# The round of a local transformer in another order: values at its head, scores in two halves

## The chip, the cores and the metric

The kernel runs on one core of a Trainium2 chip. A core has five engines that run side by side, each with its own queue of instructions: TensorE (PE, matmuls; PEld is its loading of weights), VectorE (DVE), ScalarE (ACT), GpSimd (POOL) and SyncE (SP, which issues transfers). An instruction waits in its queue until the semaphores that it names are high enough, and everything behind it on that queue waits with it. PE writes to PSUM, a memory of eight banks; DVE and ACT read results from there. The metric is the time on the device in microseconds (us), the median over runs. All times below are in us unless ns is written.

## The reference

The reference takes `x` of four sequences of 512 tokens with 128 features and adds eight blocks to it: cross attention, a mixture of experts, cross attention, a quantised feed-forward block with a convolution, a windowed cross attention, a transformer of six layers with local attention, cross attention, and a second mixture of experts. The change lies in the transformer of six layers alone. In each layer it computes (cut to what matters):

```
def attn_layer(x, Wqkv, qs, ksc, Wo):
    q, k, v = jnp.split(x @ Wqkv, 3, -1)          # 16 heads of 64
    q = l2norm(q) * qs;  k = l2norm(k) * ksc
    q = q * cos * scale + rotate_half(q) * sin * scale
    k = k * cos / scale + rotate_half(k) * sin / scale
    # windows of 32 queries, each sees its own 32 keys and the 32 before them, masked
    attn = jax.nn.softmax(8.0 * einsum(q, k), -1)
    return einsum(attn, v) @ Wo
def ffn_layer(x, g, bln, W1, b1, W2, b2):
    a, gate = jnp.split(layernorm(x, g, bln) @ W1 + b1, 2, -1)
    return a * jax.nn.gelu(gate) @ W2 + b2
for i in range(6):
    x = attn_layer(shift_tokens(x), Wqkv[i], q_scale[i], k_scale[i], Wo[i]) + x
    x = ffn_layer(shift_tokens(x), ln_g[i], ln_b[i], W1[i], b1[i], W2[i], b2[i]) + x
```

`shift_tokens` moves half of the features by one token. All of it is computed in 32-bit floats.

## The kernel before

The kernel has three stages. The first and the last (first, middle and last part) are lists of pieces that a planner puts into an order by estimated costs; the change does not touch them. Between them stands `local_transformer` (from line 1804), whose order is written out by hand: `tc.manual_schedule()` leaves each engine's instructions in the order of the program, and the framework adds the semaphores that the data, the buffers and the PSUM banks ask for.

The work is cut into tiles of 128 tokens: 6 layers x 4 sequences x 4 tiles, 96 tiles in all. The loop of line 2095 runs over rounds n. Round n works on three tiles at once: T (tile n), T1 (n-1) and T2 (n-2). Beside them runs the feed-forward block of a finished sequence (a "row" of four tiles), F, spread over four rounds, its phases 0 to 3. The parts of a round are:

- `queries_or_keys(T, kind, c)` (line 1835): a product of 128x128 with 128x512 for half c of the queries (kind 0) or keys (kind 1) into one of two banks "mm", and its squares on ACT. `rotate` (1847): on DVE two multiplications by tables of cosine and sine and a sum of the squares per head, on POOL the addition of the two. `normalise` (1868): inverse norms of queries and keys, with Ln and Exp on ACT between small steps on POOL, and then four multiplications on POOL.
- `values(T, x0)` (1905): two products into the banks "tr", copied by ACT to `v1`, and four to six transfers on SP that make the shifted copy `v2`; POOL sets a column of ones first. Averages read them two rounds later.
- `turned(T1, kind)` (1886): eight transposes on PE for queries or keys, copied by ACT. For keys, POOL first copies the last 32 columns of the tile before.
- `scores(T1)` (1932): eight matmuls that put the mask into the two banks "sc", and 128 small ones (64 rows, 32 columns, 64 wide) that add the scores. `softmax(T1)` (1955): maximum and subtraction on DVE, the exponential on ACT (line 1965).
- `probabilities(T2)` (1967): eight transposes of the exponentials. `average(T2, g)` (1972): 64 small matmuls with the values for four pairs of heads, into the banks "av"; `normalised(T2, g)` (1987) divides by the sums on DVE and frees these banks, which the next averages need. `attended(T2)` (1995): eight transposes of the averages. `project_out(T2)` (2001): sixteen matmuls into "av"; `residual(T2)` (2007) adds them to Y on DVE.
- `ff_stage(F, phase, second)` (2074): phase 0 transposes of Y and moments, and later in the round the norm on DVE (`ff_norm`); phase 1 transposes ("turn") and gates 0 and 1, whose Gelu runs on ACT; phase 2 gate 2, then ups 0 and 1 (DVE); phase 3 up 2, then the down product, which DVE adds to Y. All of these use the banks "sc", between two uses by scores.
- `swap` (2065): a copy on ACT with the halves of the features exchanged, once per row, for the products of the values.

All transposes of a tile go through `to_features` (617, on PE line 621), four to a bank "tr". ACT holds one set of function tables at a time: Gelu needs another set than Ln and Exp, and line 2084 loads the set for Ln and Exp again after gate 2. Exp alone and Ln alone also stand in sets of their own; a pass of the build puts a load before a function that the present set lacks.

The order of a round before is: first products of the queries, probabilities, second product, the feed-forward's first part, first averages, queries turned, keys' first product, second averages, keys turned, keys' second product, averages' transposes, scores, output product, values, the feed-forward's second part.

Of the kernel before, what the change touches and what calls it, by code (L numbers as in the profile page):

```python
# [21 lines left out]
F32 = mybir.dt.float32  # L22
# [4 lines left out]
ALU = mybir.AluOpType  # L27
# [3 lines left out]
NT = S // 128  # L31
# [241 lines left out]
def tile_kernel(ctx: ExitStack, tc: tile.TileContext, A: dict, out: bass.AP):  # L273
# [1530 lines left out]
    def local_transformer(Y, lf, lw, columns, tabs):  # L1804

        with ExitStack() as es:
# [21 lines left out]
            class Tile:  # L1828


                def __init__(self, i, b, tt):
                    self.i, self.b, self.tt = i, b, tt
                    self.rot, self.raw, self.ss = {}, {}, None
# [34 lines left out]
            def normalise(T):  # L1868
# [13 lines left out]
                for (kind, c), a in sorted(T.rot.items()):  # L1882
                    o = LH * kind + 8 * c
                    G.tensor_tensor(a, a, bc(y[:, o : o + 8], [128, 8, LD], 2), ALU.mult)  # L1884

            def turned(T, kind):
# [3 lines left out]
                t = qp.tile([128, LH // 2, lead + 128], F32, name="kT" if kind else "qT")  # L1890
                if kind and T.tt:
                    G.tensor_copy(t[:, :, 0:32], T.before.kT[:, :, 128:160])
                elif kind:
                    G.memset(t[:, :, 0:32], 0.0)
# [5 lines left out]
                if kind:  # L1900
                    T.kT = t
                else:
                    T.qT = t
# [28 lines left out]
            def scores(T):  # L1932

                T.banks = pair("sc").rearrange("p z (k d) -> p z k d", d=64)
                for w in range(4):
                    for z in range(2):
                        r = slice(64 * (z ^ (w // 2)), 64 * (z ^ (w // 2)) + 64)
                        PE.matmul(  # L1940
                            T.banks[32 * w : 32 * w + 32, z], identb[r, r.start : r.start + 32],
                            maskw[r, int(w + T.tt == 0)], start=True, stop=False,
                            skip_group_check=True,
                        )
                for k in range(LH // 2):
# [9 lines left out]
            def softmax(T):  # L1955

                P = tp.tile([128, LH // 2, 2, LD], F32, name="P", bufs=1)
                mx = small.tile([128, 2, LH // 2], F32, name="la_mx")
                V.tensor_reduce(mx, T.banks, AX.X, ALU.max)  # L1959
                V.tensor_tensor(  # L1960
                    P.rearrange("p k z d -> p z k d"), T.banks,
                    bc(mx, [128, 2, LH // 2, LD], 3), ALU.subtract,
                )
                T.P = P.rearrange("p k z d -> p k (z d)")
                SC.activation(T.P, T.P, AF.Exp, scale=8.0)  # L1965
# [56 lines left out]
            def ff_norm(F):  # L2022
                layernorm(F.xn, F.xn, F.found)
# [50 lines left out]
            def ff_stage(F, phase, second):  # L2074
                F.w1, F.w2 = loaded[F.i][2:]
                if phase == 0 and not second:
                    ff_moments(F)
                elif phase == 1:
                    ff_gate(F, 0, 1) if second else ff_turn(F)
                elif phase == 2 and second:  # L2080
                    ff_up(F, 0, 1)
                elif phase == 2:
                    ff_gate(F, 2)
                    SC.preload_act_table_set(EXP_LN)
                elif phase == 3:
                    ff_down(F) if second else ff_up(F, 2)

# [5 lines left out]
            for n in range(len(tiles) + 2):  # L2095
                T = tiles[n] if n < len(tiles) else None
                T1 = tiles[n - 1] if 0 <= n - 1 < len(tiles) else None
                T2 = tiles[n - 2] if 0 <= n - 2 < len(tiles) else None
                m, phase = divmod(n - 6, 4)
                F = rows[m] if 0 <= m < len(rows) else None  # L2100
                if T:
# [13 lines left out]
                    queries_or_keys(T, 0, 0)  # L2115
                if T2:
                    probabilities(T2)
                if T:
                    queries_or_keys(T, 0, 1)
                    rotate(T, 0, 0)  # L2120
                if F:
                    ff_stage(F, phase, False)
                if T2:
                    average(T2, 0)
                if T1:
                    turned(T1, 0)
                if T:
                    queries_or_keys(T, 1, 0)
                if T2:
                    normalised(T2, 0)  # L2130
                if T:
                    rotate(T, 0, 1)
                if T2:
                    average(T2, 1)
                if T1:
                    turned(T1, 1)
                if T:
                    queries_or_keys(T, 1, 1)
                if T2:
                    normalised(T2, 1)  # L2140
                if T:
                    rotate(T, 1, 0)
                if T2:
                    attended(T2)
                if T and T.tt == NT - 1 and n + 1 < len(tiles):
                    swap(tiles[n + 1].b)
                if T1:
                    scores(T1)
                if T:
                    rotate(T, 1, 1)  # L2150
                if T:
                    normalise(T)
                if T1:
                    softmax(T1)
# [144 lines left out]
```

## Time and profile before

| What | Value |
|---|---|
| Runs (three), median | 2462.42, from 2460.44 to 2462.8 |
| The profiled execution, its own time | 2456.04 |
| Its span, first to last instruction | 2454.2 |
| Mean granted clock of TensorE | 0.953 |
| Before the local transformer | 0 to 516.3 |
| Local transformer | 516.3 to 2172.4, 1656.1 long |
| After it | 2172.4 to 2454.2 |
| Busy in the local transformer | PE 1591.4, DVE 1326.7, POOL 1118.2, ACT 995.0 |
| Exponentials (line 1965) | 96, first at 541.8, last at 2157.2 |
| Loads of function tables on ACT | 55 of 1.28 each |

How to read the lines of the profile: a group names line, engine, operation, what it writes and reads by the program's names, shapes and count; then busy time and the mean of one in ns; then the idle time of the engine just before them, and what ended it. "issue" is time in which the engine waited for nothing that the profile shows. In a timeline the columns are start, length, engine, line, operation, tiles and count, with idle time before it in brackets. Matmuls are pipelined and their ends are modelled, so slots on PE are best read from start to start. q8 is the queue that moves instructions.

### The profile page before, as it was taken

To read this page: it belongs to the slowest core of one execution; us is meant where nothing else is said; L and a number is where in the kernel's file an instruction comes from. 1 tells how busy PE (TensorE), PEld (TensorE's weight loads), DVE (VectorE), ACT (ScalarE), POOL (GpSimd) and SP (SyncE) were. 2 spreads that over 40 slices of the span, in tenths; PEclk is the share of its full clock that TensorE was granted. 3 is DMA by queue.
4 is the path that set the end of the run, shared out by engine and by line. 5 is a ranking of instruction groups with operands and counts; after the bars stand their busy time and mean duration, and the time that the engine had idled before them with its cause. 6 is when DMAs were issued, how large, how long until landed. Compare 5 with 4: busy or idle time off the path is not lost. (4 is left out here: it accounts for less than half of the span.)

```text
span 2454.2 us, 86703 instructions
## 1 busy us (share of the span) xinstructions
PE 2228.0 (91%) x37341; PEld 1479.5 (60%) x37341; DVE 1759.3 (72%) x3896; ACT 1298.1 (53%) x2389; POOL 1338.6 (55%) x1862
## 2 busy tenths in 40 slices
PE   7958969978999999999999999999999999989676
PEld 3536734546666666666666666666666666644355
DVE  5545356866888888777887888887878788767422
ACT  3423325645666655666666666565666666525222
POOL 2141330256667676766667766766667666710433
PEclk9868989988999999999999999999999999989688
DMA  7201110016211121111211121111211111120023
GB/s 182 68 21 41 40 60 2 1 41 135 80 35 29 35 70 36 33 29 35 75 31 36 29 79 33 29 35 27 80 31 31 35 29 35 27 67 23 26 67 95
DMA packets 134298, 116.14 MB, mean 47 GB/s; under 512 B 29506, under 2 KB 102701, under 8 KB 133917
## 3 DMA queue, kind: packets, MB, share of 16 engines
q1 hardware_dynamic: 122037, 99.67, 15.8%
q0 software_dynamic: 4608, 7.35, 0.9%
q8 instruction: 296, 4.85, 0.9%
q10 hardware_dynamic: 7271, 3.58, 0.5%
q14 instruction: 86, 0.70, 0.1%
HBM read 42.84 MB, written 21.52 MB: 26 GB/s over the span
## 5 line engine op out<-in xcount | busy, mean ns | idle before, releaser
L1865 POOL TENSOR_TENSOR rc<-rc,rs 128x512 f32<-128x512 f32 x384 | 489.8, 1276 | 400.7 <-DVE rs L1855 326.3
L1842 PE MATMUL ps_mm<-wqk,y 128*128 128x512 f32 x768 | 397.2, 599 | 5.3 <-issue 3.5
L1884 POOL TENSOR_TENSOR rc<-rc,rn_y 128x512 f32<-128x512 f32 x384 | 388.6, 1044 | 7.5
L1852 DVE TENSOR_TENSOR rc<-ps_mm,tabs 128x512 f32<-128x512 f32 x384 | 262.5, 684 | 129.8 <-ACT sq L1844 126.5
L1844 ACT ACTIVATE sq<-ps_mm 128x512 f32<-128x512 f32 x384 | 231.2, 602 | 161.4 <-PE ps_mm L1842 108.0
L1855 DVE TENSOR_TENSOR rs<-ps_mm,tabs 128x512 f32<-128x512 f32 x384 | 261.5, 681 | 0.2 <-POOL rc L1865 0.2
L1864 DVE TENSOR_REDUCE ss<-sq 128x8 f32<-128x512 f32 x384 | 259.5, 676 | 0.0
L621 PE MATMUL ps_tr<-cst,rc 128*128 128x128 f32 x1536 | 210.9, 280 | 4.3 <-POOL rc L1884 4.0
L1980 PEld LDWEIGHTS ps_av<-v,PT 64*32 64x32 f32 x12288 | 138.1, 105 | 126.5 <-PE ps_tr L621 54.1
L2004 PE MATMUL ps_av<-aT,wo 128*128 128x128 f32 x1536 | 200.7, 283 | 2.4 <-issue 2.4
L2004 PEld LDWEIGHTS ps_av<-aT,wo 128*128 128x128 f32 x1536 | 181.0, 193 | 12.6 <-issue 3.9
L621 PEld LDWEIGHTS ps_tr<-cst,rc 128*128 128x128 f32 x1536 | 165.6, 142 | 24.4 <-POOL rc L1884 5.1
L1949 PE MATMUL ps_sc<-kT,qT 64*32 64x64 f32 x12288 | 148.1, 225 | 33.6 <-issue 32.9
L1980 PE MATMUL ps_av<-v,PT 64*32 64x65 f32 x12288 | 170.3, 225 | 6.2 <-DVE attn L1990 1.7
L1949 PEld LDWEIGHTS ps_sc<-kT,qT 64*32 64x32 f32 x12288 | 141.2, 105 | 44.2 <-issue 38.1
L1056 POOL DMA_INDIRECT back<-ye,to x80 | 78.8, 985 | 147.5 <-DVE ye L1170 104.0
L1842 PEld LDWEIGHTS ps_mm<-wqk,y 128*128 128x128 f32 x768 | 124.5, 192 | 56.3 <-issue 50.1
L1965 ACT ACTIVATE P<-P 128x1024 f32<-128x1024 f32 x96 | 101.4, 1057 | 97.3 <-DVE P L1960 97.3
L1876 ACT ACTIVATE rn_y<-ss 128x32 f32<-128x32 f32 x96 | 22.0, 229 | 237.9 <-POOL ss L1875 237.9
L802 ACT ACTIVATE P<-ps,deltaT 77x512 f32<-77x512 f32 x192 | 115.8, 683 | 56.7 <-PE ps L796 53.0
L1896 ACT COPY qT<-ps_tr 128x512 f32<-128x512 f32 x192 | 103.3, 589 | 74.6 <-PE ps_tr L621 74.3
L1959 DVE TENSOR_REDUCE la_mx<-ps_sc 128x16 f32<-128x1024 f32 x96 | 116.9, 1218 | 31.0 <-PE ps_sc L1949 31.0
(399 smaller groups left out, 4368.9 us busy)
## 6 DMA issues: line engine op xcount, KB each, us to landing
v<-v SPq DMA_DIRECT2D x432, 65.0 KB
v<-v SPq DMA_DIRECT2D x96, 195.0 KB
wqk<-in_L_ffn_Wqkv_dram SPq DMA_DIRECT2D x24, 256.0 KB
sent<-xn SPq DMA_DIRECT2D x2, 2210.0 KB
xe<-sent SPq DMA_DIRECT2D x16, 260.0 KB
back<-xn SPq DMA_DIRECT2D x2, 2048.0 KB
raw<-in_L_ffn_W_dram SPq DMA_DIRECT2D x8, 512.0 KB
w<-in_L_ffn_W_dram SPq DMA_DIRECT2D x16, 256.0 KB
```

The lines of the kernel that those rows point to most:

```text
L621: PE.transpose(t[:, i], src[:, i], ident)
L1842: PE.matmul(t, lhs, T.w[2 * kind + c], start=True, stop=True)
L1844: SC.activation(sq, t, AF.Square)
L1852: V.tensor_tensor(a, t, bc(T.tabs[:, 2 * kind, tt], [128, 8, LD], 1), ALU.mult)
L1855: V.tensor_tensor(r.rearrange("p h (x d) -> p h x d", x=2), t.rearrange("p h (x d) -> p h x d", x=2)[:, :, ::-1], bc(T.tabs[:, 2 * kind + ...
L1864: V.tensor_reduce(T.ss[:, kind, 8 * c : 8 * c + 8], sq, AX.X, ALU.add)
L1865: G.tensor_tensor(a, a, r, ALU.add)
L1884: G.tensor_tensor(a, a, bc(y[:, o : o + 8], [128, 8, LD], 2), ALU.mult)
L1949: PE.matmul(T.banks[32 * w : 32 * w + 32, z, k], T.qT[r, k, 32 * w : 32 * w + 32], T.kT[r, k, 32 * w : 32 * w + 64], start=False, stop=Tru ...
L1959: V.tensor_reduce(mx, T.banks, AX.X, ALU.max)
L1980: PE.matmul(T.means[32 * w : 32 * w + 32, x0, k], T.PT[r, 4 * g + k, 32 * w : 32 * w + 32], (T.v1 if w % 2 else T.v2)[r, x0, 4 * g + k], s ...
L2004: PE.matmul(t, T.wo[:, c], T.aT[:, c], start=(c == 0), stop=(c == 7))
```

## The change

The order of a round becomes a table of stages, `period`, each with the number of rounds by which its tile lags behind n, and a loop that runs through it.

- The values stand at the head of the round, after the first product of the queries; then comes the first product of the keys. The second product of the queries is the last of the four.
- `normalise` is split: the inverse norms stay at the end of the tile's own round, the four multiplications go to the head of the next one, on POOL behind the values' memsets. The copy of the keys of the tile before (`keys_before`) moves to the end of the round.
- The keys are turned ahead of the second averages.
- `scores` runs in two halves of four pairs of heads, with the averages' transposes between them.
- The residual moves to the head of the round after the output product (a lag of three), behind the feed-forward norm, which also moves to the head of the next round.
- The feed-forward's second part (gates 0 and 1, ups 0 and 1, down) moves from the round's end to its middle, between the keys' second product and the turning of the keys; on ACT it is then ahead of the round's Ln, Exp and exponential, on DVE ahead of the keys' second rotation.

One more round (99 for 98) drains the longer lag. No operation of the reference is added or left out. The diff, cut to its core:

```diff
-            def normalise(T):
+            def inverse_norms(T):
...
-                for (kind, c), a in sorted(T.rot.items()):
-                    o = LH * kind + 8 * c
-                    G.tensor_tensor(a, a, bc(y[:, o : o + 8], [128, 8, LD], 2), ALU.mult)
+                T.inv = y
+            def normalise(T, kind):
+                for c in range(2):
+                    a, o = T.rot[kind, c], LH * kind + 8 * c
+                    G.tensor_tensor(a, a, bc(T.inv[:, o : o + 8], [128, 8, LD], 2), ALU.mult)
             def turned(T, kind):
                 lead = 32 * kind
-                t = qp.tile([128, LH // 2, lead + 128], F32, name="kT" if kind else "qT")
-                if kind and T.tt:
-                    G.tensor_copy(t[:, :, 0:32], T.before.kT[:, :, 128:160])
-                elif kind:
-                    G.memset(t[:, :, 0:32], 0.0)
+                t = T.kT if kind else qp.tile([128, LH // 2, 128], F32, name="qT")
                 for c in range(2):
                     SC.copy(
                         t[:, 4 * c : 4 * c + 4, lead:],
                         to_features(T.rot[kind, c].rearrange("p (k x) d -> p k (x d)", x=2)),
                     )
-                if kind:
-                    T.kT = t
+                T.qT = T.qT if kind else t
+            def keys_before(T):
+                T.kT = qp.tile([128, LH // 2, 160], F32, name="kT")
+                if T.tt:
+                    G.tensor_copy(T.kT[:, :, 0:32], T.before.kT[:, :, 128:160])
                 else:
-                    T.qT = t
+                    G.memset(T.kT[:, :, 0:32], 0.0)
...
-            def scores(T):
...
-                for k in range(LH // 2):
+            def scores(T, g):
+                if g == 0:
+                    T.banks = pair("sc").rearrange("p z (k d) -> p z k d", d=64)
...
+                for k in range(4 * g, 4 * g + 4):
...
-            def softmax(T):
+            def largest(T):
+                T.mx = small.tile([128, 2, LH // 2], F32, name="la_mx")
+                V.tensor_reduce(T.mx, T.banks, AX.X, ALU.max)
+            def exponentials(T):
                 P = tp.tile([128, LH // 2, 2, LD], F32, name="P", bufs=1)
-                mx = small.tile([128, 2, LH // 2], F32, name="la_mx")
-                V.tensor_reduce(mx, T.banks, AX.X, ALU.max)
                 V.tensor_tensor(
                     P.rearrange("p k z d -> p z k d"), T.banks,
-                    bc(mx, [128, 2, LH // 2, LD], 3), ALU.subtract,
+                    bc(T.mx, [128, 2, LH // 2, LD], 3), ALU.subtract,
...
-            def ff_norm(F):
-                layernorm(F.xn, F.xn, F.found)
+            def ff_norm(F, phase):
+                if phase == 0:
+                    layernorm(F.xn, F.xn, F.found)
...
-            def ff_stage(F, phase, second):
-                F.w1, F.w2 = loaded[F.i][2:]
-                if phase == 0 and not second:
+            def ff_first(F, phase):
+                if phase == 0:
                     ff_moments(F)
                 elif phase == 1:
-                    ff_gate(F, 0, 1) if second else ff_turn(F)
-                elif phase == 2 and second:
-                    ff_up(F, 0, 1)
+                    ff_turn(F)
                 elif phase == 2:
                     ff_gate(F, 2)
                     SC.preload_act_table_set(EXP_LN)
+                else:
+                    ff_up(F, 2)
+            def ff_second(F, phase):
+                if phase == 1:
+                    ff_gate(F, 0, 1)
+                elif phase == 2:
+                    ff_up(F, 0, 1)
                 elif phase == 3:
-                    ff_down(F) if second else ff_up(F, 2)
+                    ff_down(F)
+            period = (
+                (ff_norm, 1),
+                (queries_or_keys, 0, 0, 0),
+                (values, 0, 0),
+                (values, 0, 1),
+                (residual, 3),
+                (queries_or_keys, 0, 1, 0),
+                (probabilities, 2),
+                (normalise, 1, 0),
+                (normalise, 1, 1),
+                (rotate, 0, 0, 0),
+                (rotate, 0, 1, 0),
+                (ff_first, 0),
+                (average, 2, 0),
+                (turned, 1, 0),
+                (queries_or_keys, 0, 1, 1),
+                (normalised, 2, 0),
+                (ff_second, 0),
+                (turned, 1, 1),
+                (average, 2, 1),
+                (rotate, 0, 1, 1),
+                (queries_or_keys, 0, 0, 1),
+                (normalised, 2, 1),
+                (scores, 1, 0),
+                (attended, 2),
+                (rotate, 0, 0, 1),
+                (scores, 1, 1),
+                (largest, 1),
+                (project_out, 2),
+                (inverse_norms, 0),
+                (keys_before, 0),
+                (exponentials, 1),
+            )
+            by_row = (ff_first, ff_norm, ff_second)
...
-            for n in range(len(tiles) + 2):
+            for n in range(len(tiles) + 3):
...
-                    queries_or_keys(T, 0, 0)
-                if T2:
-                    probabilities(T2)
-                if T:
-                    queries_or_keys(T, 0, 1)
...
-                if F and phase == 0:
-                    ff_norm(F)
-                if T:
-                    values(T, 0)
-                    values(T, 1)
-                if F:
-                    ff_stage(F, phase, True)
+                for stage, lag, *which in period:
+                    if stage in by_row:
+                        m, phase = divmod(n - lag - 6, 4)
+                        if 0 <= m < len(rows) - 1:
+                            F = rows[m]
+                            F.w1, F.w2 = loaded[F.i][2:]
+                            stage(F, phase)
+                    elif 0 <= n - lag < len(tiles):
+                        stage(tiles[n - lag], *which)
+                    if stage is attended and T and T.tt == NT - 1 and n + 1 < len(tiles):
+                        swap(tiles[n + 1].b)
```

More of the change, by code (lines that the diff above doesn't have):

```diff
@@ L1832, in __init__ @@
                     self.i, self.b, self.tt = i, b, tt
-                    self.rot, self.raw, self.ss = {}, {}, None
+                    self.rot, self.raw, self.ss, self.qT = {}, {}, None, None
             def queries_or_keys(T, kind, c):
@@ L1930, in values @@
                         DMA.dma_start(T.v2[64:96, 1], T.before.v1[32:64, 1])
-            def scores(T):
[L1936 to L1944, printed above, removed]
-                for k in range(LH // 2):
+            def scores(T, g):
+                if g == 0:
+                    T.banks = pair("sc").rearrange("p z (k d) -> p z k d", d=64)
+                    for w in range(4):
+                        for z in range(2):
+                            r = slice(64 * (z ^ (w // 2)), 64 * (z ^ (w // 2)) + 64)
+                            PE.matmul(
+                                T.banks[32 * w : 32 * w + 32, z],
+                                identb[r, r.start : r.start + 32],
+                                maskw[r, int(w + T.tt == 0)], start=True, stop=False,
+                                skip_group_check=True,
+                            )
+                for k in range(4 * g, 4 * g + 4):
                     for w in range(4):
@@ L2084, in ff_stage @@
                     SC.preload_act_table_set(EXP_LN)
-                elif phase == 3:
-                    ff_down(F) if second else ff_up(F, 2)
+                else:
[5 more added lines that the diff above has]
+                    ff_up(F, 0, 1)
+                elif phase == 3:
+                    ff_down(F)
[31 more added lines that the diff above has]
+                (exponentials, 1),
+            )
+            by_row = (ff_first, ff_norm, ff_second)
             tiles = [Tile(i, b, tt) for i in range(DEPTH) for b in range(B) for tt in range(NT)]
@@ L2094, in local_transformer @@
             SC.preload_act_table_set(EXP_LN)
-            for n in range(len(tiles) + 2):
+            for n in range(len(tiles) + 3):
                 T = tiles[n] if n < len(tiles) else None
[L2097 to L2100, printed above, removed]
                 if T:
@@ L2114, in local_transformer @@
                     T.tabs = tabs[T.i]
-                    queries_or_keys(T, 0, 0)
-                if T2:
-                    probabilities(T2)
-                if T:
-                    queries_or_keys(T, 0, 1)
-                    rotate(T, 0, 0)
-                if F:
[L2122 to L2126, printed above, removed]
-                if T:
[L2128 to L2154, printed above, removed]
-                if T2:
-                    project_out(T2)
-                    residual(T2)
-                if F and phase == 0:
-                    ff_norm(F)
-                if T:
-                    values(T, 0)
-                    values(T, 1)
-                if F:
-                    ff_stage(F, phase, True)
+                for stage, lag, *which in period:
[9 more added lines that the diff above has]
+                        swap(tiles[n + 1].b)
             return loaded[DEPTH - 1][2:]
```

## The prediction

> **What bounds the kernel now.** I read the page first, then the busy time by stage, the waits, and the timeline of single rounds.
>
> ```profile
> PE 2228.0 (91%) x37341; PEld 1479.5 (60%) x37341; DVE 1759.3 (72%) x3896; ACT 1298.1 (53%) x2389; POOL 1338.6 (55%) x1862
> ...
> q8 instruction: 296, 4.85, 0.9%
> ```
>
> ```profile
> 516.30:2172.40 1656.10, 1591.40 (x31702) 1078.85 (x31702) 1326.71 (x2331) 995.00 (x1817) 1118.22 (x1574) 0.99 0.18 45
> ```
>
> The second fence is the stage of the local transformer (columns: length, then busy time of PE, PEld, DVE, ACT, POOL, then clock). All edits lie in it. PE is busy 96% of it at a clock of 0.99, so PE's issue order sets the time; other engines matter only where PE waits. L1965 starts from 541.8 to 2157.2, 96 times: 17.0 a round, 68.0 for the four rounds of a row. I call them A (moments), B (turn, gates 0 and 1), C (gate 2, ups 0 and 1) and D (up 2, down).
>
> ```profile
> PE ps_sc L1949 <- issue: 32.9, 31, 2.2
> PE ps_tr L621 <- ACT v L1920: 5.4, 15, 1.4
> ```
>
> ```profile
> 1233.00 0.41 PE L1940 MATMUL ps_sc<-maskw,identb 64*32 64x512 bf16 x8
> 1233.22 1.27 PE L1949 MATMUL ps_sc<-kT,qT 64*32 64x64 f32 x107
> 1235.69 0.42 PE L1949 MATMUL ps_sc<-kT,qT 64*32 64x64 f32 x21 [1.20 <-issue]
> 1236.04 2.05 PE L2004 MATMUL ps_av<-aT,wo 128*128 128x128 f32 x16
> ...
> 1249.51 0.41 PE L1940 MATMUL ps_sc<-maskw,identb 64*32 64x512 bf16 x8
> 1249.74 1.46 PE L1949 MATMUL ps_sc<-kT,qT 64*32 64x64 f32 x128
> 1251.12 2.05 PE L2004 MATMUL ps_av<-aT,wo 128*128 128x128 f32 x16
> ```
>
> PE's largest wait names no other engine: the score loop stops for "issue". At 1233 it breaks off after 107 matmuls and resumes 1.2 later; a round on it runs through.
>
> **Step 1, the score loop in two halves.** By its starts the loop takes 1.24 in 64 of 96 rounds, 1.27 and 1.34 in two, and 2.1 to 5.5 in 30; the excess is 41, without the one of 5.5 in the fill 36.8. Counted in the trace, the breaks lie 1280, 2048, 3328 or 5376 PE instructions apart, all multiples of 256, and q8 moved 296 packets of 16 KB: one per 256 instructions. PE resumes 2.2 to 2.7 (median 2.4) after the last q8 packet started. So a block of 256 PE instructions that runs in less than some 2.45 us makes PE wait for the next. Masks, loads and scores are 272 instructions in 1.46. After the change the densest 256 are a half of scores (128 in 0.77 with the switch behind it), the averages' transposes (16 in 0.96) and 112 of the other half (0.54): 2.27; with the second averages, a product, masks and scores it is 2.49. A stall is then at most 0.2; at the present rate I put 0.15 a row, 3.6. The term is -33 (bounds 0, if the stall has another cause, and -36.8).
> The Trainium skill (Runtime: NRT & Kernel Launch, section Instruction fetch mechanics) says that instructions come in blocks of 256, as the trace shows, but that fetching is hidden because dispatch is slower than the fill. By that rule this term is 0, and the sum below would be +23.6, 2486; the 32.9 us under "issue" speak against it.
>
> **Step 2, PE's own slots.** Start to start in the rounds from 1223 to 1293: a product (two matmuls) 0.86, eight transposes 0.87 (0.93 for q and k, 0.96 before masks or scores), 64 averages 0.80, masks 0.22, scores 1.38 with their exit, output product 1.88; entering averages or masks from a product or from transposes costs 0.09 more. Before, a round without feed-forward is 14.01. After: scores 0.77+0.76 for 1.38 (+0.15), and the keys' transposes now stand before averages (+0.09): 14.25. 96 x 0.24 = +23 (bounds 0 and +38, at 0.4; the exit from averages into a product is in no row, so I take that into transposes, 0.15).
> Check: 4 x 14.01, feed-forward 9.01 (0.53, 0.59, 1.71, 0.95, 1.71, 0.95, 2.57), breaks 36.8/24 = 1.53, and waits seen in a row 1.27 (second averages in A 0.22, turn in B 0.41, attended transposes in C 0.44, averages behind squares 0.2) give 67.85 for 68.0.
>
> **Step 3, waits that go and come.** With 0 at the start of a round's first product, its own order gives: values to 2.58, keys' first product to 3.44, P's transposes to 4.31, feed-forward, first averages, and so on. The maximum starts 0.19 after the output product, subtract ends 2.67 after it: 0.8 in the next round. ACT: exponential to 1.8, square, two value copies (to 2.9 and 3.4), square, PT copies from 4.15; P's second group needs the second value copy at 3.87, so 0.4 is spare. POOL (normalise, 4.05, now at the head) has the queries done at 4.1, wanted at 5.6 or later; the values' memsets (0.13, 0.52, 0.52) ahead of it add 1.05 in the first round of a row of tiles, and still fit. The values' four to six DMAs move to the head of SP's queue; their readers come two rounds later, and weight loads behind them are eight rounds ahead.
> Round A: no wait. Round B: residual now stands behind the feed-forward norm on DVE (four L559, 3.78): done 5.25, and the first averages need its bank at 4.96: 0.35 with the turn. Round D:
>
> ```profile
> 1220.87 2.74 PE L2062 MATMUL ps_sc<-fh,lw 128*128 128x512 f32 x6
> ...
> 1223.64 1.52 DVE L1826 SCALAR_TENSOR_TENSOR y<-ps_sc,cols,y 64x512 f32<-64x512 f32 x2 [3.22 <-PE ps_sc L2062]
> ```
>
> DVE's add to Y waits 2.77 for the down product, takes 1.5, and now stands ahead of a rotation (1.79) and the second normalised (0.9): 7.0 after the down product's start, while PE reaches the second group of the averages' transposes at 6.75: 0.28. In round C the same with the ups: 0.1. Round C also gets this:
>
> ```profile
> 1256.35 1.28 ACT L2042 ACT_TABLE_LOAD   x1
> 1257.64 1.27 ACT L2042 ACTIVATE fh<-ps_sc,cols 128x512 f32<-128x512 f32 x2
> ...
> 1261.43 1.28 ACT L2084 ACT_TABLE_LOAD   x1
> 1262.72 1.07 ACT L1896 COPY qT<-ps_tr 128x512 f32<-128x512 f32 x2
> ```
>
> Gates 0 and 1 move ahead of the round's Ln, Exp and exponential. The built order of the changed kernel has a table load before L1876 and another before L1877 in every round B, and one more before gate 2 in C: five a row for two, 69 more in all. In B: swap ends at 15.6, load to 16.9, Ln, load to 18.45, Exp, exponential from 18.7, which is 1.76 in C instead of 0.83. Value copies end at 3.8 and 4.3, P's transposes are late by 0.5. In C, two loads round gate 2's Gelu hold the queries' copies to 9.1; the keys' transposes need their banks at 10.1: covered, by 0.4.
> New waits 0.35 + 0.5 + 0.1 + 0.28 = 1.23 for 1.27: -1 over 23 rows (bounds -29, all hidden, and +23, one more us a row).
> The Trainium skill (ScalarE: Activation LUTs, section What ACT_TABLE_LOAD costs) gives a load 1283 ns and a drain of 1380 ns with it. By that the two loads in B's chain would take 2.76 more, 23 x 2.76 = +63, so 2516. The rows agree on the load; Gelu starts 1.29 after it, so they show no drain.
>
> **Step 4, ends.** The weights of the first values are issued at 515.1 and their packets run to 518.7, while the first product starts at 516.36: the values at the head hold the second product by some 2. In the drain, normalising the last tile waits at the head of its round (+1.8), while the last down product no longer follows the last output product (-1.4): +2 together (bounds 0 and 5).
>
> **Sum.** -33 + 23 - 1 + 2 = -9. The profiled execution took 2456.04 (span 2454.2), so 2447; it stood 6.4 under the median of the runs, so the runs should show 2453.
>
> **The rivals.**
> *The exponential comes later than I have it* (slower). ACT in round B is nearly full: some 14.7 of 16.9 us with its three loads, and Ln, Exp and the exponential are last in its queue. For it: "ACT rn_y L1876 <- POOL ss L1875" is a wait of 2.3 to 2.4 a round already. Against: that wait covers the first load. Each us of delay is one us of PE in round C, 23 in all; from 0.6 the change is slower than before by more than noise. At one us: 2476.
> *The breaks stay* (slower), because they follow the fetch and not the density: 2486. Against: they are in the score loop and nearly nowhere else, where 64 averages run.
> *A load costs a drain*: 2516; no row shows one.
> *The halves cost more switches*: 0.4 a round for 0.24 gives +15 on the sum less what waits absorb: about 2463, no change.
> That the order is not what the title says is excluded: the built order shows the halves, and apart from the loads no engine gets another instruction.
>
> **Chances.** Forecast (2435 to 2457): 0.45. No change, within 0.2% or 5 us, which is about what the measurement can tell: 0.15. Late exponential: 0.25. Breaks stay: 0.12. Drain: 0.03. Faster 0.45, same 0.15, slower 0.40. The range goes from 2435, where the new waits are hidden and the breaks gone, to 2487, where the breaks stay; outside lie some 0.15. The forecast's own range is 2440 to 2462.
>
> **What would show it.** Right: "issue" before the scores' matmuls falls from 33 to under 5; 124 table loads for 55; in a row, P's transposes wait about 0.5 in C; PE's stage is about 1647. Wrong: breaks in the score halves, or a wait of PE on ACT of more than 1 in each round C.

## The result and the profile after

| | before | after |
|---|---|---|
| Median of the runs (13 each, side by side) | 2463.92 | 2455.09 |
| The profiled execution, its own time | 2456.04 | 2455.09 |
| Its span | 2454.2 | 2453.2 |
| First to last exponential | 1615.4 | 1613.3 |
| 22 rows of four tiles (the second to the 23rd), mean | 68.08 | 67.90 |
| The shortest rows | 66.3 | 67.4 |

The ratio of the runs is 0.9963, with a 95% interval from 0.9948 to 0.9978: the changed kernel is faster by about 0.4%. A second comparison later, on another chip, gave 0.9974 (0.9957 to 0.9990). The forecast of the median, 2453, was within 2.1, and the side (faster) was right. On the profiled execution alone the forecast was 2447, and that one took 2455.1. Both halves of this, the gain that came and the gain that did not, are taken apart below.

The page of the changed kernel, engine by engine, and the queue that moves instructions:

```profile
PE 2264.2 (92%) x37341; PEld 1494.4 (61%) x37341; DVE 1736.0 (71%) x3896; ACT 1390.5 (57%) x2458; POOL 1326.0 (54%) x1862
...
q8 instruction: 296, 4.85, 0.8%
```

The same instructions on every engine, apart from 69 more on ACT: the table loads. The stretch of the local transformer, with the same columns as before (the transformer of the changed kernel itself runs from 517.5 to 2170.5):

```profile
516.30:2172.40 1656.10, 1622.93 (x31709) 1091.17 (x31709) 1304.88 (x2331) 1088.59 (x1888) 1105.26 (x1574) 0.99 0.17 45
```

PE is busy for 31.5 more than before with as many matmuls. So about half of what was idle time has become slots. The waits of PE in that stretch:

```profile
PE ps_sc L1954 <- issue: 7.3, 6, 4.3
PE ps_tr L621 <- ACT P L1971: 5.1, 2, 3.3
PE ps_tr L621 <- POOL rc L1887: 3.6, 3, 3.1
```

The largest wait of before, 32.9 in 31 pieces ahead of the scores, has become 7.3 in 6 pieces, of which 4.3 is one break in the fill. A round as PE now runs it (columns: start, length, engine, line, tiles, count):

```profile
1252.03 1.13 PE L1842 MATMUL ps_mm<-wqk,y 128*128 128x512 f32 x2
1253.09 0.41 PE L1944 MATMUL ps_sc<-maskw,identb 64*32 64x512 bf16 x8
1253.32 0.84 PE L1954 MATMUL ps_sc<-kT,qT 64*32 64x64 f32 x64
1254.09 1.09 PE L621 MATMUL ps_tr<-cst,attn 128*128 128x128 f32 x8
1255.12 0.86 PE L1954 MATMUL ps_sc<-kT,qT 64*32 64x64 f32 x64
1255.90 2.05 PE L2010 MATMUL ps_av<-aT,wo 128*128 128x128 f32 x16
```

From start to start the halves take 0.77 and 0.78, the transposes between them 1.03, and no break is left.

**Where the time went.** PE's instructions come in blocks of 256. At each boundary of a block one can measure the time from the start of the last instruction of one block to the start of the first of the next; call it a stall where it is over 0.2. The table leaves out the ordinary step of 0.43 from one matmul of a product to the next. These stalls and the rest of a row, from the traces of both comparisons:

| | before | after | before, 2nd chip | after, 2nd chip |
|---|---|---|---|---|
| Mean row | 68.08 | 67.90 | 67.99 | 67.81 |
| Stalls at boundaries in 22 rows | 41.0 (39) | 8.3 (12) | 43.1 (48) | 7.5 (12) |
| Row without its stalls | 66.2 | 67.5 | 66.0 | 67.5 |
| First product to first exponential | 25.4 | 27.8 | 25.5 | 28.0 |
| Last exponential to last matmul | 13.6 | 11.9 | 13.6 | 11.9 |
| First product to last matmul | 1654.5 | 1653.0 | 1650.7 | 1648.8 |

In 22 rows 32.7 of stalls go (35.6 in the second pair), and everything else grows by 1.3 to 1.4 a row, some 29 to 32. That leaves -4.0 in the rows in both pairs. The fill up to the first exponential takes 2.3 to 2.5 of it back and the first row another 2.2 to 2.5; the three rounds behind the 22 rows give 0.5 to 0.9 and the drain 1.7. So the transformer is 1.5 to 1.9 shorter by these traces.

Of the signs that the prediction had named, the 124 table loads came. "Issue" before the scores fell to 7.3 and not under 5, though 4.3 of it lies in the fill. From the first product to the first matmul behind it the stage took 1656.2 before and 1653.8 after, not 1647.

### The profile page after: what moved, and what is told of

It is laid out like the page before. It is cut to its first block, busy times and chain, and to the rows that moved or that the text cites. A ratio compares the mean times of both kernels' runs of the same rounds, so it can differ in the third digit from the quotient of the medians.

```text
span 2453.2 us, 86604 instructions
## 1 busy us (share of the span) xinstructions
PE 2264.2 (92%) x37341; PEld 1494.4 (61%) x37341; DVE 1736.0 (71%) x3896; ACT 1390.5 (57%) x2458; POOL 1326.0 (54%) x1862
## 5 line engine op out<-in xcount | busy, mean ns | idle before, releaser
L1842 PE MATMUL ps_mm<-wqk,y 128*128 128x512 f32 x768 | 405.1, 609 | 3.2 <-DVE rs L1855 1.8
L621 PEld LDWEIGHTS ps_tr<-cst,rc 128*128 128x128 f32 x1536 | 173.7, 142 | 66.2 <-issue 51.4
L1986 PEld LDWEIGHTS ps_av<-v,PT 64*32 64x32 f32 x12288 | 137.6, 105 | 66.2 <-ACT PT L1976 47.2
L1954 PE MATMUL ps_sc<-kT,qT 64*32 64x64 f32 x12288 | 165.9, 224 | 7.3 <-issue 7.3
L2005 ACT COPY aT<-ps_tr 128x512 f32<-128x512 f32 x192 | 106.8, 587 | 113.0 <-PE ps_tr L621 112.9
L1954 PEld LDWEIGHTS ps_sc<-kT,qT 64*32 64x32 f32 x12288 | 147.6, 105 | 30.5 <-issue 25.2
L1996 DVE TENSOR_TENSOR attn<-ps_av,la_den 128x512 f32<-128x512 f32 x192 | 132.8, 692 | 6.6
```

The costliest lines, as they stand in the source:

```text
L621: PE.transpose(t[:, i], src[:, i], ident)
L1842: PE.matmul(t, lhs, T.w[2 * kind + c], start=True, stop=True)
L1954: PE.matmul(T.banks[32 * w : 32 * w + 32, z, k], T.qT[r, k, 32 * w : 32 * w + 32], T.kT[r, k, 32 * w : 32 * w + 64], start=False, stop=Tru ...
L1986: PE.matmul(T.means[32 * w : 32 * w + 32, x0, k], T.PT[r, 4 * g + k, 32 * w : 32 * w + 32], (T.v1 if w % 2 else T.v2)[r, x0, 4 * g + k], s ...
L1996: V.tensor_tensor(T.attn[:, 4 * g : 4 * g + 4].rearrange("p k x d -> p x k d"), T.means[:, :, :, 0:LD], bc(den, [128, 2, 4, LD], 3), ALU.mult,
```

## The experiments

The experiments ran on other chips than the first comparison; there the kernel before took 2409 to 2417, so ratios to it are what counts. "Stalls" below is the sum over the boundaries in the whole local transformer, 53.5 in the kernel before and 16.0 in the changed one (2.5 and 0.9 of it are ordinary steps of products). The twelve runs in one view:

```
                              ratio to before (95%)      stalls  first to last exponential
before again                  0.9989 (0.9974 to 1.0004)   55.7   1611.6
changed, again                0.9974 (0.9957 to 0.9990)   15.1   1608.9
halves alone                  0.9996 (0.9975 to 1.0017)   33.0   1620.7
changed, scores in one piece  1.0257 (1.0226 to 1.0288)   57.1   1686.5
values at head alone          1.0343 (1.0319 to 1.0368)   39.4   1695.7
changed, values at the tail   1.0737 (1.0713 to 1.0761)   15.1   1793.0
before, shifted by 128        0.9997 (0.9981 to 1.0014)   55.6   1614.7
changed, shifted by 128       0.9998 (0.9980 to 1.0017)   19.6   1614.6
changed, shifted by 64        0.9967 (0.9954 to 0.9981)   13.1   1607.9
changed, one load by hand     0.9943 (0.9922 to 0.9965)   19.7   1606.3
changed, rotation ahead       0.9932 (0.9910 to 0.9953)   18.6   1607.5
changed, both of these        0.9932 (0.9908 to 0.9957)   16.0   1597.1
```

### Only the halves

```diff
-            def scores(T):
+            def scores(T, g):
...
+                if T1:
+                    scores(T1, 0)
                 if T2:
                     attended(T2)
...
-                    scores(T1)
+                    scores(T1, 1)
```

> The kernel before with one part of the change alone: the scores run in two halves of four pairs of heads, with the averages' transposes between them; everything else keeps its old place. Theory (dense blocks of 256 instructions make PE wait for the next block): the breaks inside the score loop go (issue before the scores' matmuls falls from 33 to under 7), for which each round pays 0.15 to 0.24 of switches on PE, 14 to 23 in all; a row of four tiles takes 67.2 to 67.5 instead of 68.1, and the time is 10 to 22 below the kernel before (ratio 0.991 to 0.996). Rival (the breaks follow the count of instructions, wherever the dense part stands): issue stays above 25 and the time is 0 to 23 above the kernel before (ratio 1.000 to 1.009).

Neither came: stalls fell to 33.0, and the time did not move. The waits of PE in this kernel, and one of the breaks that are left:

```profile
PE ps_sc L1950 <- issue: 15.8, 25, 3.2
...
PE ps_sc L1950 <- POOL kT L1892: 3.8, 5, 0.8
```

```profile
1050.11 1.09 PE L621 MATMUL ps_tr<-cst,attn 128*128 128x128 f32 x8
1051.13 0.81 PE L1950 MATMUL ps_sc<-kT,qT 64*32 64x64 f32 x59
1052.24 0.31 PE L1950 MATMUL ps_sc<-kT,qT 64*32 64x64 f32 x5 [0.29 <-issue]
```

The second half still breaks, here for 0.5. An undisturbed row is 67.16 against 66.3, so the halves cost 0.2 a round on PE: 88 rounds of it are 19, and the stalls of the 22 rows fell by 20 (41.0 to 20.8). The two cancel.

What the prediction had too simple is the length that a block needs. It said 2.45, the time from the start of the q8 packet to PE's resuming. But the packet does not always start with the block. Over the kernel before, the k-th packet starts a median of 1.0 after PE enters the k-th block, and brings the block after it. So a block has to run for this delay and the 2.45. In the kernel before, the short blocks that begin in masks or scores had a delay of -0.2 to 0.4, so 2.45 fitted them: those that ran for 1.4 to 2.2 stalled by 0.2 to 1.3, those that ran for 2.4 to 2.8 by no more than 0.14. In this experiment the 17 blocks of the 22 rows that begin in masks or scores and ran for 2.4 to 3.2 had packets 0.4 to 1.4 late, and they stalled by 0.1 to 1.3. Blocks of the same place and length in both kernels:

```
                block begins     ran   packet starts after   stall at its end
halves alone    at 1049.3       2.39    +0.43                 0.51
                at 1185.0       2.54    +0.82                 0.70
                at 1918.6       2.41    +0.68                 0.78
changed         at 1152.2       2.69    -0.27                 0.00
                at 1508.2       2.52    -0.36                 0.00
                at 1643.7       2.37    -0.42                 0.01
```

The blocks run equally long, so density does not separate the two: in the changed kernel the packet starts some 0.3 before PE has crossed the boundary, and it starts ahead of it in 15 of the 16 blocks that begin in masks or scores and run for less than 2.9. What brings it forward was not isolated. In the experiment the keys' copy on ACT ends 0.35 before the scores that need it (1048.99 and 1049.34), in the changed kernel 1.2 before (1235.3 and 1236.55), so PE's queue may stand at that wait in the one and run ahead in the other; that is a guess.

### The changed kernel with the scores in one piece

```diff
-                (scores, 1, 0),
                 (attended, 2),
                 (rotate, 0, 0, 1),
+                (scores, 1, 0),
                 (scores, 1, 1),
```

> The changed kernel with both halves of the scores at the place of the second one, behind the averages' transposes, so that the masks, loads and 128 scores are one dense block again. Theory (density): the breaks come back in about a third of the rounds, issue before the scores' matmuls rises from 7 to 30 or more, less 0.15 of a switch a round (14): 13 to 25 above the changed kernel, so 0.9995 to 1.007 of the kernel before. Rival (the gain came from the other moves, the halves only cost): 0 to 14 below the changed kernel, ratio 0.990 to 0.996 of the kernel before.

The stalls came back as expected (57.1), but the kernel became slower than the changed one by about 70 (1.0257 for 0.9974), some three times what was expected. PE's waits name the reason:

```profile
PE ps_tr L621 <- DVE attn L1996: 64.7, 70, 1.3
PE ps_sc L1954 <- issue: 35.1, 25, 2.2
```

In the changed order nothing but a product, 1.06, stands between the second averages and their transposes if the first half is taken away. DVE's division by the sums (0.2 and 0.69, behind what it has in hand) does not fit in there. The first half of the scores has a second job: it covers that division.

### The values, moved alone and left alone

The changed kernel with the values back behind the output product:

```diff
                 (queries_or_keys, 0, 0, 0),
-                (values, 0, 0),
-                (values, 0, 1),
...
                 (project_out, 2),
+                (values, 0, 0),
+                (values, 0, 1),
```

> The changed kernel with one part undone: the values' two products, copies and transfers stand behind the output product again. Theory (the transfers of the shifted copies run while a block of instructions is fetched, and its packet starts 2.6 after the boundary, not 1.0): the stalls at boundaries rise from 16 to 25 or more, and the time is 8 to 20 above the changed kernel, less the 2 to 3 of the fill that come back. Rival (the transfers don't matter): stalls stay at 16 and the time is 0 to 4 below the changed kernel.

Both theories fell. The stalls stayed, so nothing shows that the transfers matter to them in this order (rows are 8 longer here, so the test is a weak one); yet the time rose by 7%:

```profile
PE ps_tr L621 <- ACT P L1971: 82.5, 88, 3.0
...
ACT v L1924 <- PE ps_tr L1923: 289.0, 178, 4.7
```

ACT's copies of the values now stand ahead of the exponential on ACT's queue and wait for products at the end of the round. The exponential waits behind them, and P's transposes wait for the exponential in nearly every round (88 times; a row is 75.9). This is the largest wait, 82.5 of the some 180 that the rounds grew by; the rest was not taken apart.

And the kernel before, with the values at the head:

```diff
                     queries_or_keys(T, 0, 0)
+                    values(T, 0)
+                    values(T, 1)
                 if T2:
                     probabilities(T2)
...
-                if T:
-                    values(T, 0)
-                    values(T, 1)
```

> The kernel before with one part of the change alone: the values stand at the head of the round, behind the first product of the queries. Theory (transfers against fetch): of the 53 of stalls at boundaries, the 24 of blocks that ran for 3.9 to 4.5 fall by half or more, the 12 of score loops that fill a block stay; with 2 to 3 more in the fill the time is 5 to 15 below the kernel before, ratio 0.994 to 0.998. Rival: stalls of 50 or more, ratio 1.000 to 1.003.

The part on stalls came out: of the 23.8 that the blocks of 3.9 to 4.5 held in the kernel before, 11.3 are left, the 12 us of the shortest blocks stay (14.1), and the sum falls to 39.4. In the kernel before 19 of these 60 blocks stalled; 14 of the 19 had a packet 2.5 to 3 late, and in 13 of these some 50 to 210 packets of q1, the queue of the values' copies among others, started in just that time. Both fit a collision but do not prove it, as the moved values give PE new waits too. And the kernel is slower by 3.4%:

```profile
PE ps_tr L621 <- ACT v L1920: 22.1, 62, 0.8
PE ps_sc L2039 <- DVE P L1960: 21.5, 22, 1.3
PE ps_sc L2062 <- DVE P L1960: 14.9, 21, 0.9
PE ps_sc L2050 <- DVE P L1960: 12.9, 20, 0.7
```

In the old order the two products of the values kept PE busy after the output product, while DVE's subtraction freed the score banks that gates, ups and down product need next. Without them PE waits, 49.3 in all. In the change these products moved and the feed-forward's second part moved away from that place too.

The changed kernel lost the stalls of such blocks in another way: it has few of them. Blocks that run for 3.9 to 4.5 number 60 in the kernel before (57 and 59 in its other two traces), 37 with the halves alone, 17 in the changed kernel (14 to 18 in its other three) and 14 with the values back at the tail.

### Where the boundaries fall

A row is 10.5 blocks long, so boundaries come back to nearly the same places every two rows, and the fall in stalls might be luck. Idle matmuls in the first tile's masks shift every later boundary:

```diff
-                    for w in range(4):
+                    for w in [0, 1, 2, 3] * (9 if T is tiles[0] else 1):
                         for z in range(2):
```

> The kernel before with 64 idle matmuls (128 instructions with their loads, some 1.8 us) in the first tile's masks, which write what the first mask then overwrites: every later boundary between two blocks of 256 instructions falls half a block further on. Theory (density: the loop of 272 instructions in 1.46 stalls wherever the boundary falls in it): the stalls at boundaries add up to 45 to 60, as before (53), and the time is 0 to 8 above the kernel before (ratio 1.000 to 1.004). Rival (the stalls are an accident of where the boundaries fall, which recur every two rows): they change by more than 20, and the time by more than 0.8%.

> The changed kernel with the same 128 idle instructions in the first tile's masks. Theory (density): the stalls at boundaries stay between 10 and 25 (16 in the changed kernel), the time 0 to 6 above the changed kernel, 0.996 to 0.9985 of the kernel before. Rival (an accident: the changed kernel's boundaries happen to fall well): the stalls rise to 35 or more, the time by 20 or more, ratio above 1.004.

> The changed kernel with 64 idle instructions in the first tile's masks, a quarter of a block. Density: stalls at boundaries of 12 to 24, 0 to 5 above the changed kernel (0.9 of it the idle matmuls themselves). Accident of the boundaries' places: stalls of 30 or more, 15 or more above the changed kernel.

In stalls there is no luck: 55.6 for 53.5 before, 19.6 and 13.1 for 16.0 after. The undisturbed row of the changed kernel stays at 67.4 in all three. In the time the shift by 64 is as expected: 2403.04, with 2403.20 for the changed kernel unshifted, in the same comparison. The shift by 128 came out at 0.9998, above its expected range, on a chip where the changed kernel did not run unshifted. So in this pair, 0.9997 and 0.9998, no gain shows in the time. Of the 6 to 8 that separate it from 0.9974 or 0.9963, 3.6 of stalls are one part; the idle matmuls are no other, since the first exponential follows the first product after 27.7, and after 27.8 without them. Its interval overlaps that of the second comparison and just misses that of the first. What else differs stays open.

### The second load of tables

The build puts a load ahead of Ln and another ahead of Exp. One load by hand of the set with both takes their place:

```diff
+            def both_tables(F, phase):
+                if phase == 1:
+                    SC.preload_act_table_set(EXP_LN)
...
                 (project_out, 2),
+                (both_tables, 0),
                 (inverse_norms, 0),
```

> The changed kernel with one load of the set that holds both Ln and Exp, put by hand ahead of the inverse norms in the feed-forward's round B; it takes the place of the two that the build put ahead of Ln and of Exp. Theory (the second load delays the exponential, and with it P's transposes in round C): round C is 0.5 shorter, a row 66.9 instead of 67.4, 23 x 0.5 = 11 below the changed kernel (ratio to the kernel before about 0.992). Rival (ACT has that time to spare): the same time as the changed kernel within 3, ratio 0.996, with 23 loads of tables fewer.

An undisturbed row falls from 67.41 to 67.09: round B, up to the exponential, is 0.84 shorter and round C, behind it, 0.54 longer (counted from first product to first product, round C takes 17.18 for 17.48). So the second load did delay P's transposes, by 0.32 where 0.5 was expected. ACT's queue in the changed kernel at that place:

```profile
1256.39 1.28 ACT L1876 ACT_TABLE_LOAD   x1
1257.69 0.23 ACT L1876 ACTIVATE rn_y<-ss 128x32 f32<-128x32 f32 x1
1257.94 1.28 ACT L1877 ACT_TABLE_LOAD   x1
1259.23 0.23 ACT L1877 ACTIVATE rn_y<-rn_y 128x32 f32<-128x32 f32 x1
1259.37 1.04 ACT L1971 ACTIVATE P<-P 128x1024 f32<-128x1024 f32 x1
```

And in the kernel with both improvements, in the same round:

```profile
1227.14 1.28 ACT L1870 ACT_TABLE_LOAD   x1
1228.43 0.23 ACT L1880 ACTIVATE rn_y<-ss 128x32 f32<-128x32 f32 x1
1228.69 0.23 ACT L1881 ACTIVATE rn_y<-rn_y 128x32 f32<-128x32 f32 x1
1229.27 1.06 ACT L1975 ACTIVATE P<-P 128x1024 f32<-128x1024 f32 x1 [0.35 <-DVE P L1970]
```

With one load the exponential's last releaser is DVE's subtraction again: that is why only part of the 1.28 is gained.

The Trainium skill (ScalarE: Activation LUTs, section Table sets: the hidden batching unit) says that Ln and then Exp take one load, since a set holds both. The trace agrees that this set serves both, but not that it is taken unasked: 23 loads stand ahead of L1876 and 23 ahead of L1877 in the changed kernel.

### The addition to Y in round D

```diff
             def ff_down(F):
...
+                    if F.with_:
+                        rotate(F.with_, 1, 1)
...
-                (rotate, 0, 1, 1),
+                (rotate_late, 0),
...
+                            F.with_ = T
```

In round D alone DVE rotates the keys' second half before the addition to Y; `rotate_late` does it in the other rounds.

> The changed kernel with one step moved, in round D alone: on DVE the rotation of the keys' second half stands ahead of the down product's addition to Y, not behind it. Theory (the addition waits 2.8 for the down product and holds the rotation and the second normalised behind it, so that the second group of the averages' transposes is late by 0.28): round D falls from 18.27 to 18.0, 23 x 0.28 = 6 below the changed kernel. Rival (the transposes do not wait for it): the same time within 2.

Round D falls by 0.42 (18.27 to 17.85), round A gives 0.09 back, and the row is 67.08, 0.33 less. What stood there in the changed kernel, on DVE:

```profile
1285.89 1.51 DVE L1826 SCALAR_TENSOR_TENSOR y<-ps_sc,cols,y 64x512 f32<-64x512 f32 x2 [2.98 <-PE ps_sc L2069]
1287.44 0.69 DVE L1852 TENSOR_TENSOR rc<-ps_mm,tabs 128x512 f32<-128x512 f32 x1
...
1290.08 0.68 DVE L1852 TENSOR_TENSOR rc<-ps_mm,tabs 128x512 f32<-128x512 f32 x1
```

DVE idles for 2.98 in front of the addition, with the rotation behind it ready to run. The transposes of the averages take 1.36 from start to start in that round and 1.02 in A.

### Both improvements, and both kernels again

> The changed kernel with both improvements: one load by hand of the set with Ln and Exp in round B for the build's two, and in round D the keys' second rotation ahead of the addition to Y. If the two are independent (each took 0.32 from a row): an undisturbed row of 66.8, 23 x 0.64 = 15 below the changed kernel, ratio 0.989 to 0.993. If they share one slack: a row of 67.1 and 7 below.

> The kernel before as it is, with a trace of its own on the chip of the next three. If the earlier trace (2456.0, some 8 under the median of its runs) was of a quick execution: rows of 68.1 again on the mean, stalls at boundaries of 50 to 58, and the profiled time at or above its runs' median. If the traces of two executions differ as much as the two kernels do: rows outside 67.9 to 68.3. The ratio is 1 within 0.2%.

> The changed kernel as it is. Theory: rows of 67.4 where no block stalls and 67.9 on the mean, stalls at boundaries of 14 to 20, ratio 0.995 to 0.998 as before. Rival (the first ratio owed something to its chip or its runs): 0.999 to 1.001.

The two are independent: the undisturbed row is 66.75 (67.41 less 0.32 and 0.33), and from the first to the last exponential it takes 1597.1 where the changed kernel took 1608.9 beside it, 11.8 less. By the medians it is 2396.06 against 2403.20, 7 less and about half of the 15 that were expected, and 0.9932 (0.9908 to 0.9957) of the kernel before: the fastest kernel here by median and by trace, though its interval still overlaps that of the changed kernel and matches that of the moved rotation alone.

The kernel before repeated itself (rows of 67.99, stalls of 55.7, 0.9989), and so did the changed one. Of what was expected of the first trace the part on rows and stalls came true; but the profiled execution was again some 4 under its median (2404.65 with 2408.54), while that of the changed kernel stood at its median (2404.12 with 2403.20). So both pairs of traces show a span 0.5 to 1.0 shorter, and both pairs of medians a gain of 6 to 9. One trace is one execution, and its span holds more than the change: outside the local transformer, where nothing was edited, the four traces of the last comparison take 751.0 to 758.4. So the spans of a pair cannot settle a few us, and the stage itself, 1.5 and 1.9 shorter, is the better measure. The medians gain more than that; why stays open.

## Why the prediction was right, and where it was not

**Step 1, the score loop (-33).** Right in size: stalls in 22 rows went from 41.0 to 8.3, that is -32.7, and they hardly depend on where the boundaries fall. The reason was right in part. Dense code does outrun the fetch of the next block; with the scores in one piece the stalls return. But the limit of 2.45 leaves out the delay of the packet. It fitted the short blocks of the kernel before, whose delay was -0.2 to 0.4. It called the blocks of some 4 us safe, which held 23.8 of the 53.5, mostly behind packets that were 2.5 to 3 late. And with the halves alone the short blocks' packets start 0.4 to 1.4 late, so that half of the stalls stay. The rest went in the new order because the packets of the short blocks start earlier and because few blocks of 4 us are left (17 for 60); which of its moves does this was not isolated. That the values' transfers hold packets up is supported in the old order alone, where moving the values took 12 from the blocks of 4 us; in the new order moving them back brought no stalls. Residual stalls of 0.15 a row were put down; 0.38 a row came.

On the Trainium skill (Runtime: NRT & Kernel Launch, section Instruction fetch mechanics), whose rule would have made this term 0: blocks of 256 and a queue of PE's own agree with 296 packets of 16 KB; that the fetch is hidden does not, with 41 of stalls in 22 rows of the one kernel and 8 in those of the other.

**Step 2, PE's own slots (+23).** This is the term that was mis-sized. Start to start, a round without its feed-forward part and waits takes 14.3 to 14.5, on the mean some 14.40, where 14.25 was worked out: +0.39 a round and not +0.24, so +37 over 96, at the upper bound that was given (+38). The difference is in two places that the rounds of before do not have: the product between the averages and the masks (1.05 for 0.95, start to start) and the transposes between two score halves (1.03 for 0.96).

**Step 3, the waits (-1).** The list was right in three of four places. P's transposes in round C start 0.19 late and lose 0.11 more inside, 0.30 for 0.5; the averages' transposes lose 0.34 in D (0.28) and 0.11 in C (0.1). The fourth, the residual behind the feed-forward norm in B (0.35), is not there in an undisturbed row: the norm ended 2.7 after the round's first product, not 3.78, and the residual 3.2 after it. But in 8 of the 22 rows the same place in B, the norm's transposes, the first averages and the queries' transposes, loses 0.2 to 0.7; where a row names what ended the wait it is mostly ACT's copies of P's transposes or POOL's multiplications, and not the residual. That is 0.17 a row on the mean (0.14 in the second pair). New waits of 0.75 in an undisturbed row and 0.92 on the mean, for 1.23, make this term -8 and not -1, and offset half of what step 2 missed. Both of the larger waits were confirmed by taking away their cause: 0.32 and 0.33 a row.

**Step 4, the ends (+2).** The first exponential is 2.3 later after the first product, about as forecast. In the drain the last output product follows the last exponential 0.9 later, where 1.8 was put down. But the last down product, which ended 2.6 behind the last output product, now ends 5.1 ahead of it, so the last matmul comes 1.7 earlier after the last exponential. Together that is +0.6, within the bounds. The first row grew by 2.2 to 2.5, which is more than the steps put on a row.

**The sum.** Predicted -9 on the profiled execution, seen -1.0; predicted -9.4 on the median, seen -8.8. The rows had been forecast at -33 and 4 x 0.24 - 0.04 = 0.92 a row of other cost; they show -32.7 and 1.3. That is 8 more over 22 rows, about the gap of the traced pair. Of the 1.3, the slots make 4 x 0.39 and the waits 0.92 - 1.27, together 1.21; the rest is in neither. That the forecast of the median hit is in large part luck: its terms came out at -1.5 to -1.9 in the traces of the stage, and the 4 to 7 by which the medians gained more are in no step. The lower end of the range, 2435, does not follow from the bounds either: 29 of waits hidden and 36.8 of breaks gone would give some 2421.

**The rivals.** The late exponential was right as a mechanism (it starts 1.58 into round C, with 1.76 forecast) and wrong in price: 0.32 a row, not one us. The breaks did not stay. No drain shows: Ln starts 1.30 after its load starts, and the next load 1.55 after the first. More switches than 0.24 a round is what happened, at 0.39 nearly the 0.4 of that rival, whose 2463 the smaller waits kept away in part.

## What to carry to other kernels

Where the profile calls a wait "issue" in the middle of a loop of small matmuls, count instructions between the breaks: at multiples of 256 it was the fetch of the next block here, and a block had to run for the delay of its packet and some 2.45 more. The delay was 1.0 on the median here but moved from -0.4 to 3 with the order of the work, so it has to be read in the trace of the new order. A stage moved in a tuned order gives up its cover: two of these moves, made or undone alone, cost 3% and 7%, and the single piece of scores another 3%, each through a wait that was small or absent in the first profile. Where PE loses a little in the same place of every row, look at what stands first in the queues of DVE and ACT there: the two best edits here put ready work ahead of an instruction that waits, and one table load in the place of two.

## What the runs showed that was not expected

The packet that brings the next block starts not at the boundary but 1.0 later on the median; 2.5 to 3 later ahead of most stalls of blocks of some 4 us, some 4.0 later behind many of the short blocks that stalled, and up to 2.5 before the boundary in the changed kernel. Stalls at boundaries moved between 13 and 57 in kernels with nearly the same PE instructions. The two parts of this change that were made alone are worth nothing or a loss (0.9996 and 1.0343). The whole is worth 0.3 to 0.4% in two comparisons and did not show in the pair that was shifted by 128.
